# A two-layer Mamba and attention kernel: the state scan's B factor through PSUM, half of its C product on GpSimd

## The chip, the cores and the metric

One core of one Trainium2 chip runs the whole program. The metric is the device time of one execution in microseconds (us), the median of the runs shown.

## The reference, cut to what matters

The input x has shape (2, 2048, 256). It passes two layers, each `x = x + s * g`. In the first layer s is a Mamba block with a GELU feed-forward behind it, and g is the SiLU of a SwiGLU block with blockwise FP4 rounding. In the second, s is an attention over a length of 2 with 16 heads, and g is the SiLU of a chain of three blocks of linear layers with low-rank parts. The change concerns the Mamba scan, with 512 inner channels and 16 states:

```
def step(h, inp):
    dt_t, B_t, C_t, x_t = inp
    dA = jnp.exp(dt_t[..., None] * A)
    h = dA * h + dt_t[..., None] * B_t[:, None, :] * x_t[..., None]
    y = jnp.sum(h * C_t[:, None, :], axis=-1)
    return (h, y)
...
y = ys.transpose(1, 0, 2) + D * xc
y = y * _silu(z)
return y @ out_proj_w
```

B_t and C_t have 16 values for each time step, the same for all channels; they come out of a projection of xc (`x_proj_w`).

## The kernel before

The sequence is cut into 16 chunks (u = 0 to 15) of 128 time steps for both batch rows, so a chunk has T = 256 columns. Channels lie on the partitions, 512 of them as four groups m of 128. For a chunk, `head` does the layer norm, the input projection, the convolution (as matmuls with diagonal matrices, `cdiag`), the projection to dt, B and C, and the product `ux` = dt * xc. `scan` follows; `fp4_half` and `tail` do the FP4 block and the feed-forward; `second` is the whole second layer of the chunk.

`scan` goes through the 16 states in pairs: 8 steps a chunk, 128 in all. B and C were written to a small tensor in device memory (`bc`), and each step loads both, broadcast to all partitions, in one transfer (`bcs`, 128 x 1024 values). ScalarE makes `decay` = exp(dt * A) in 8 instructions. VectorE does three long instructions on 2048 columns: `hh` = ux * B, then `tensor_tensor_scan` over decay and hh, then `hh` = hh * C. TensorE sums over the states: 16 transposes of hh against the identity for each step accumulate in the two PSUM banks `y`. When all steps are done, y is multiplied with silu(z), transposed back and projected (`sz`, `y2`, `po`). `hh` and `bcs` have two buffers each.

None of this is issued where it is written. `Recorder` records every operation with its engine; a planner inside the kernel then gives each a cost and a start time, goes forward and backward through all of them in several passes with keys from two lists (`adjust`, `passes`), takes the buffers of each tag in turn, and `issue` emits the result as one fixed order for each engine. So all instructions of the kernel carry one line of the profile (L579 before; the same statement is L605 in the changed file), and they are told apart by tile names. Each engine works through its own list in order; an instruction that waits holds all that stand behind it. Loads and stores stand in the list of SyncE (SP). GpSimd (POOL) does almost nothing: `ident`, some memsets, and the inverse roots of the layer norms, `tensor_tensor` with `pow` on 2 or 4 columns (`ln_sq`, `ln_y`).

The eight PSUM banks are dealt out by `BANKS` and `USES`: two for y, two for `m` (head and the end of scan), two for `f` (FP4 and feed-forward), one for `s` and one for `h` (second layer).

Of the kernel before, what the change touches and what calls it, by code (L numbers as in the profile page):

```python
# [29 lines left out]
BANKS = {"y": 2, "m": 2, "f": 2, "s": 1, "h": 1}  # L30
USES = {
    "q": "f", "s0": "s", "s1": "s", "h0": "h", "h1": "h",
    "e0": "m", "e1": "y", "g0": "h", "g1": "f",
# [8 lines left out]
class Recorder:  # L42
# [69 lines left out]
    def cost(self, engine, method, args, kwargs):  # L112
# [6 lines left out]
        if engine == "gpsimd":  # L119
            if method == "memset":  # L120
                return 0.04
            return 0.69 if method == "tensor_tensor" else 0.19
# [88 lines left out]
    def prepare(self):  # L211
# [12 lines left out]
        for i, (engine, method, args, kwargs, stage) in enumerate(ops):  # L224
# [14 lines left out]
            if engine == "gpsimd":  # L239
                self.table[i] = int(method != "memset")  # L240
            if engine == "sync":
                self.size[i] = 2 if args[0].dtype == BF16 else 4
                for d in args[0].shape:
                    self.size[i] *= d
            if engine == "scalar" and method == "activation":
                func = str(args[2]).rsplit(".", 1)[-1]
                self.table[i] = self.TABLES.get(func, 0)
# [41 lines left out]
    def backward(self, unit, bonus, ahead):  # L289
# [7 lines left out]
        def transfer(i):  # L297
            return size[i] / self.RATE if engine[i] == "sync" else 0.0
# [68 lines left out]
    def forward(self, key, bonus, ahead):  # L367
# [10 lines left out]
        warm, upto, moved, kind = False, 0, 0.0, 0  # L378
        tags, lines, turn, opened_of = {}, {}, {}, {}
# [53 lines left out]
        while done < n:  # L433
            best_e, best_t = None, 1e18
            for e, c in cand.items():
                if c:
                    f = free[e]
                    m = min(ready[i] for i in c)
                    t = f if f > m else m
                    if t < best_t:  # L440
                        best_e, best_t = e, t
# [5 lines left out]
            for i in c:  # L447
                if ready[i] <= limit:
                    k = key[i]
                    if ready[i] > best_t:  # L450
                        k -= (ready[i] - best_t) * 0.3
# [6 lines left out]
            t = max(free[best_e], ready[i])  # L458
# [4 lines left out]
            if best_e == "gpsimd" and table[i]:  # L463

                t = max(t, free["vector"])
# [22 lines left out]
            if best_e == "sync":  # L488

                moved = max(moved, t + cost) + self.size[i] / self.RATE  # L490
                stop = moved + tails["sync"]
# [91 lines left out]
def tile_two_layers(ctx: ExitStack, tc: tile.TileContext, a: dict):  # L583
# [53 lines left out]
    def load_x(u):  # L637
        t = io.tile([P, B, D], F32, tag="xt", name=f"xt_{u}")
# [12 lines left out]
    w_xp = const.tile([P, 4, 2, 2, R], F32, tag="w_xp", name="w_xp")  # L651
    xpw = a["x_proj_w"].rearrange("(c p) (s f) -> p c s f", p=P, s=3)
    for q in range(2):
        rec.sync.dma_start(w_xp[:, :, q, 0, :], xpw[:, :, 0, :])
        rec.sync.dma_start(w_xp[:, :, q, 1, :], xpw[:, :, 1 + q, :])
# [57 lines left out]
    ddiag = const.tile([P, 4, P], F32, name="ddiag")  # L713
    for m in range(4):
        rec.vector.tensor_scalar(ddiag[:, m, :], ident, dvec[:, m : m + 1], None, ALU.mult)
    state = const.tile([P, NS, 4, B], F32, name="state")

# [123 lines left out]
    def load_second():  # L841
        wt["qkv"] = load("w_qkv", [P, 2, 3 * D], a["qkv_w"].rearrange("(c p) f -> p c f", p=P))

        rec.vector.tensor_scalar(
            wt["qkv"][:, :, 2 * D :], wt["qkv"][:, :, 2 * D :], 0.5, None, ALU.mult
        )
# [14 lines left out]
    def make_qlora_weights():  # L861

        scl = load("q_scl", [P, 6, 2, D // BLK], a["scales"].rearrange("i (c p) n -> p i c n", p=P))
        wl = const.tile([P, 6, 2, D], F32, tag="w_l", name="w_l")
        for i in range(6):
            qi = tmp.tile([P, 2, D], I32, tag="t2k_s0", name=f"qi_{i}", bufs=depth["s0"])
            rec.sync.dma_start(qi, a["qweights"][i].rearrange("(c p) d -> p c d", p=P))
            lab = t2k("s0", f"lab_{i}")
# [5 lines left out]
            for c in range(2):  # L874
                wv = w[:, c, :].rearrange("p (n k) -> p n k", k=BLK)
                rec.vector.tensor_tensor(
                    wv, wv, scl[:, i, c, :].unsqueeze(2).to_broadcast([P, D // BLK, BLK]), ALU.mult
# [23 lines left out]
    def head(u, xt):  # L901
# [51 lines left out]
        for m in range(4):  # L953
            rec.tensor.matmul(
                pd[: 4 * R, :T], lhsT=w_xp[:, m].rearrange("p a b r -> p (a b r)"), rhs=xc[:, m, :],
                start=(m == 0), stop=(m == 3),
            )
        xdbl = mam.tile([4 * R, T], F32, tag="xdbl", name=f"xdbl_{nm}", bufs=1)
        rec.scalar.copy(xdbl, pd[: 4 * R, :T])
        bc = dram.tile([2 * NS, T], F32, tag="bc", name=f"bc_{nm}")  # L960
        for q in range(2):
            rec.sync.dma_start(bc[q * NS : (q + 1) * NS, :], xdbl[(2 * q + 1) * R : (2 * q + 2) * R, :])
# [17 lines left out]
        return dict(xt=xt, xn=xn, lnt=lnt, xc=xc, dt=dt, ux=ux, bc=bc)  # L980

    def scan(u, h):
# [3 lines left out]
        y = [bank("y", f"y_{nm}_{g}") for g in range(TG)]  # L986
        for g in range(TG):
            for m in range(4):
                rec.tensor.matmul(
                    y[g][:, m * P : (m + 1) * P], lhsT=h["xc"][:, m, g * P : (g + 1) * P],  # L990
                    rhs=ddiag[:, m, :], start=(m == 0), stop=False, skip_group_check=True,
                )
        bcv = h["bc"].rearrange("(s n) t -> s n t", s=2)
        for n in range(0, NS, 2):

            bcs = scn.tile([P, 2, 2, T], F32, tag="bcs", name=f"bcs_{nm}_{n}", bufs=2)
            rec.sync.dma_start(bcs, bcv[:, n : n + 2, :].partition_broadcast(P))
# [9 lines left out]
            bn = bcs[:, 0].unsqueeze(2).to_broadcast([P, 2, 4, T])  # L1007
            cn = bcs[:, 1].unsqueeze(2).to_broadcast([P, 2, 4, T])
# [18 lines left out]
            rec.vector.tensor_tensor(hv[:, :, :P], hv[:, :, 1:], cn, ALU.mult)  # L1027
            for k in range(2):
                for g in range(TG):
                    for m in range(4):  # L1030
                        rec.tensor.matmul(
                            y[g][:, m * P : (m + 1) * P],
                            lhsT=hh[:, k, m, g, :P],
                            rhs=ident, is_transpose=True, start=False, stop=(n + k == NS - 1),
                            skip_group_check=True,
                        )

        y2 = [None] * TG
        for g in range(TG):
            pz = bank("m", f"pz_{nm}_{g}")  # L1040
            for c in range(2):
                rec.tensor.matmul(
                    pz, lhsT=h["lnt"][:, c, g * P : (g + 1) * P], rhs=w_in[:, c, DI : 2 * DI],
                    start=(c == 0), stop=(c == 1),
                )
            sz = scn.tile([P, DI], F32, tag="sz", name=f"sz_{nm}_{g}", bufs=1)
            rec.scalar.activation(sz, pz, AF.Silu)
            rec.vector.tensor_tensor(sz, y[g], sz, ALU.mult)
            pt = bank("m", f"py_{nm}_{g}").rearrange("p (m t) -> p m t", m=4)
            for m in range(4):  # L1050
                rec.tensor.transpose(pt[:, m, :], sz[:, m * P : (m + 1) * P], ident)
            y2[g] = t2k("m", f"y2_{nm}_{g}").rearrange("p (m t) -> p m t", m=4)
            rec.scalar.copy(y2[g], pt)
        po = bank("m", f"po_{nm}").rearrange("p (g d) -> p g d", g=TG)
        for g in range(TG):
            for m in range(4):
                rec.tensor.matmul(
                    po[:, g, :], lhsT=y2[g][:, m, :],
# [49 lines left out]
    def tail(u, h, x2, sgs, x1):  # L1108
# [37 lines left out]
        for g in range(TG):  # L1146
            sg = sgs[g]
            rec.vector.tensor_tensor(sg, sg, s[:, g, :], ALU.mult)
            rec.vector.tensor_tensor(x1[:, g, :], sg, h["xt"][:, g, :], ALU.add)


    def second(u, xv):
# [44 lines left out]
        rec.scalar.copy(dkv, pdkv)  # L1197
# [5 lines left out]
        bias_row(vm, 32, 2 * D, D)  # L1203
        for c in range(2):
            for bb in range(B):
                rec.tensor.matmul(
                    vm, lhsT=ht[:, c, bb * P : (bb + 1) * P], rhs=wt["qkv"][:, c, 2 * D :],
                    start=False, stop=(c == 1 and bb == B - 1),
                )
# [7 lines left out]
        rec.scalar.activation(e, e, AF.Tanh, scale=0.5 * float(BLK) ** -0.5)  # L1217
        for s in range(2):
            cs = ct[:, s * D : (s + 1) * D]
            rec.vector.tensor_tensor(  # L1220
                cs.rearrange("p (h d) -> p h d", d=BLK),
                dkv[:, D : 2 * D].rearrange("p (h d) -> p h d", d=BLK),
                e[:, s * NS : (s + 1) * NS].unsqueeze(2).to_broadcast([P, NS, BLK]), ALU.mult,
# [90 lines left out]
    for u in range(NU):  # L1314
# [9 lines left out]
        x1 = mam.tile([P, B, D], F32, tag="x1", name=f"x1_{u}")  # L1324
        tail(u, h, x2, sgs, x1)
        rec.stage = (u, SECOND)
        if u == 0:
# [6 lines left out]
        (3, 1, 2.23), (9, 3, -0.03), (15, 4, 1.53), (5, 1, -1.64), (13, 0, 0.68), (14, 4, -2.53),  # L1334
        (3, 3, -0.31), (14, 1, 0.96), (6, 2, -0.01), (11, 4, 1.22), (14, 2, 1), (11, 1, 0.05),
        (8, 0, 0.01), (2, 1, -2.41), (13, 1, 2.14), (3, 2, 0.51), (6, 3, 1.05), (0, 1, 1.16),
        (11, 0, -0.47), (5, 3, -1.29), (14, 0, 0.2), (13, 4, -0.85), (7, 2, 0.99), (12, 1, 0.89),
        (13, 3, -0.99), (1, 2, 0.28), (15, 1, 2.77), (14, 3, -1.39), (8, 1, 0.09), (7, 3, -0.25),
        (15, 3, 1.61), (6, 1, 0.87),
    ]  # L1340
    passes = [
        (20.0, 0.3, 0.0, 1.02, 0.1, [
            (9, 4, -0.033), (9, 1, 0.008), (4, 2, "gpsimd", -0.309), (1, 3, "tensor", 0.016),
            (2, 1, "gpsimd", 0.015), (1, 4, "vector", -0.12), (7, 3, "scalar", -0.018),
            (7, 3, "vector", 0.085), (1, 2, "gpsimd", 0.027), (1, 1, "gpsimd", -0.003),
            (9, 4, "gpsimd", 0.128), (11, 1, "vector", -0.088), (3, 4, "gpsimd", -0.076),
            (15, 4, "vector", 0.027), (1, 2, "scalar", -0.075), (8, 0, "vector", 0.016),
            (15, 3, "scalar", -0.469), (7, 3, -0.043), (13, 0, "vector", -0.017),
            (4, 3, "gpsimd", -0.036), (6, 4, 0.029), (8, 2, "vector", 0.849),
            (7, 0, "vector", -0.277), (9, 1, "vector", 0.009), (8, 2, "gpsimd", -0.192),  # L1350
            (1, 3, "gpsimd", -0.014), (0, 0, -0.03), (1, 1, "scalar", -0.005), (15, 2, 0.008),
            (3, 2, "scalar", 0.081), (7, 4, 0.045), (8, 3, 0.119), (2, 0, "tensor", -0.001),
# [184 lines left out]
```

## Time and profile before

| what | value |
|---|---|
| median of 3 runs | 1725.03 us (1724.42, 1725.03, 1729.31) |
| the profiled execution, its own time | 1715.39 us |
| its span, first to last instruction | 1713.5 us |
| mean granted TensorE clock | 0.963 |
| busy: VectorE, TensorE, ScalarE, GpSimd | 1614.3, 1552.3, 1419.4, 183.5 us |
| moved by DMA | 87.75 MB, 51 GB/s over the span |

The profile names the engines PE (TensorE; PEld is its weight load), DVE (VectorE), ACT (ScalarE), POOL (GpSimd) and SP (SyncE). A group is written engine, operation, out<-in, shapes and count; after the bar its busy time and the mean of one instruction in ns, and after the next bar how long the engine was idle just before these instructions and what ended that. Rows of a timeline begin with the start and the duration in us; where a row stands for x2, the duration is that of both.

### The profile page before, as it was taken

What the parts mean: (1) busy time and instruction counts of PE and PEld (TensorE: products, weight loads), DVE (VectorE), ACT (ScalarE), POOL (GpSimd) and SP (SyncE); (2) the same over time, 40 slices, a digit from 0 to 9 for tenths busy, and PEclk for the clock granted to TensorE, in tenths of its full rate; (3) what the DMA queues carried; (4) which work ended last, traced back from release to release, by engine and by line L of the source; (5) the groups of instructions that cost most, each with busy time, mean ns of one, the idle gap of its engine ahead of it and who ended that gap; (6) DMA issues with size and microseconds to landing.
All of it is one profiled execution on the core that took longest, in us unless ns stands there. A gap on an engine that the chain in (4) does not pass through costs nothing.

```text
span 1713.5 us, 21982 instructions
## 1 busy us (share of the span) xinstructions
PE 1552.3 (91%) x7948; PEld 1224.1 (71%) x7948; DVE 1614.3 (94%) x1638; ACT 1419.4 (83%) x2885; POOL 183.5 (11%) x114
## 2 busy tenths in 40 slices
PE   7736989999899999989999998999989899998997
PEld 5535758678687867768687876878677686867775
DVE  8999999999999999999999999999998999999932
ACT  5636877989899899899989898999978898897734
POOL 0000002001011201020102011001130101100100
PEclk9858989999999999999999999999999999999999
DMA  7322222313222232222222331222222132211000
GB/s 188 92 46 51 50 46 46 61 32 57 57 46 47 47 63 38 44 58 50 53 47 47 57 58 32 51 64 38 57 44 46 44 51 51 51 44 50 25 7 13
DMA packets 310666, 87.75 MB, mean 51 GB/s; under 512 B 262775, under 2 KB 276765, under 8 KB 310558
## 3 DMA queue, kind: packets, MB, share of 16 engines
q1 hardware_dynamic: 310558, 86.36, 25.5%
q8 instruction: 62, 1.02, 0.2%
q14 instruction: 46, 0.38, 0.1%
HBM read 80.62 MB, written 4.72 MB: 50 GB/s over the span
## 4 chain that ended last, share of the span: by engine, by line
PE 41%; ACT 20%; DVE 9%; issue 3%; POOL 1%; DMA 0%; POOLq 0%; ACTq 0%; SPq 0%; DVEq 0%
PE bank_f L579 16%; PE bank_m L579 8%; PE bank_s L579 7%; ACT decay L579 7%; PE bank_y L579 6%; ACT L579 6%; DVE hh L579 4%; ACT t2k_s L579 3%; PE bank_h L579 2%; DVE fp_l L579 2%; ACT t2k_f L579 1%; DVE t2k_s L579 1%; ACT dt L579 1%; POOL ln_sq_s L579 1%; ACT fp_h L579 0%
## 5 line engine op out<-in xcount | busy, mean ns | idle before, releaser
L579 DVE TENSOR_TENSOR_SCAN hh<-decay,hh 128x2064 f32<-128x2064 f32 x128 | 569.7, 4451 | 1.4 <-DVE ln_m_m L579 0.4
L579 ACT ACTIVATE decay<-dt,amat 128x256 f32<-128x256 f32 x1024 | 437.5, 500 | 34.3 <-DVE hh L579 33.0
L579 ACT ACT_TABLE_LOAD x313 | 401.6, 1283 | 16.5 <-DVE hh L579 3.9
L579 PE MATMUL bank_y<-ident,hh 128*128 128x128 f32 x2048 | 279.8, 283 | 36.1 <-DVE hh L579 36.1
L579 PEld LDWEIGHTS bank_y<-ident,hh 128*128 128x128 f32 x2048 | 246.6, 147 | 72.1 <-issue 47.1
L579 DVE TENSOR_TENSOR hh<-ux,bcs 128x2048 f32<-128x2048 f32 x128 | 291.8, 2279 | 6.7 <-PE bank_y L579 6.5
L579 DVE TENSOR_TENSOR hh<-hh,bcs 128x2048 f32<-128x2048 f32 x128 | 291.9, 2281 | 0.1
L579 POOL TENSOR_TENSOR ln_sq_s<-ln_sq_s,power 128x2 f32<-128x2 f32 x45 | 86.9, 1932 | 755.2 <-ACT ln_sq_s L579 755.2
L579 PE MATMUL bank_f<-w_f,t2k_f 128*128 128x256 f32 x512 | 133.6, 388 | 11.4 <-ACT t2k_f L579 11.3
L579 PE MATMUL bank_f<-t2k_f,w_f 128*128 128x256 f32 x512 | 127.6, 389 | 4.0 <-ACT t2k_f L579 3.3
L579 PE MATMUL bank_m<-xi,cdiag 128*128 128x256 f32 x512 | 124.8, 378 | 0.0
L579 PEld LDWEIGHTS bank_f<-w_f,t2k_f 128*128 128x128 f32 x512 | 94.3, 193 | 30.7 <-ACT t2k_f L579 17.6
L579 PEld LDWEIGHTS bank_f<-t2k_f,w_f 128*128 128x128 f32 x512 | 97.8, 194 | 21.7 <-ACT t2k_f L579 6.2
L579 PEld LDWEIGHTS bank_m<-xi,cdiag 128*128 128x128 f32 x512 | 93.6, 189 | 14.2 <-issue 0.5
L579 PE MATMUL bank_h<-t2k_s,w_l 128*128 128x256 f32 x360 | 92.0, 390 | 8.6 <-ACT t2k_s L579 8.6
L579 PE MATMUL bank_f<-w_down,hq 128*128 128x256 f32 x384 | 93.1, 386 | 6.7 <-ACT hq L579 6.5
L579 DVE SCALAR_TENSOR_TENSOR fp_l<-fp_h,fp_l 128x704 f32<-128x704 f32 (+2 forms) x124 | 91.8, 740 | 6.8 <-ACT fp_h L579 6.4
L579 PE MATMUL bank_f<-w_up,t2k_f 128*128 128x352 f32 x256 | 91.4, 475 | 6.0 <-ACT sg L579 2.9
L579 PE MATMUL bank_s<-w_qkv,t2k_s 128*128 128x256 f32 (+1 forms) x300 | 90.8, 430 | 4.1 <-DVE t2k_s L579 4.1
L579 PE MATMUL bank_f<-w_gate,t2k_f 128*128 128x352 f32 x256 | 90.0, 471 | 2.0 <-ACT h L579 2.0
L579 PE MATMUL bank_s<-w_l,t2k_s 128*128 128x256 f32 x360 | 89.3, 381 | 0.6 <-ACT t2k_s L579 0.6
L579 PEld LDWEIGHTS bank_f<-w_down,hq 128*128 128x128 f32 x384 | 71.6, 192 | 22.3 <-ACT hq L579 11.5
(172 smaller groups left out, 2434.2 us busy)
## 6 DMA issues: line engine op xcount, KB each, us to landing
bcs<-bc SPq DMA_DIRECT2D x128, 512.0 KB, 4.9
xt<-in_x_dram SPq DMA_DIRECT2D x16, 256.0 KB, 3.8
out_dram<-t2k_s SPq DMA_DIRECT2D x15, 256.0 KB, 2.2
w_f<-in_ffn_w_dram SPq DMA_DIRECT2D x2, 1024.0 KB
state<-hh SPq DMA_DIRECT2D x120, 8.0 KB, 2.9
t2k_s<-in_qweights_dram SPq DMA_DIRECT2D x6, 256.0 KB, 3.1
w_in<-in_in_proj_w_dram SPq DMA_DIRECT2D x1, 1024.0 KB, 5.1
h<-in_w_gate_dram SPq DMA_DIRECT2D x6, 128.0 KB
```

The source lines that it names most:

```text
L579: getattr(getattr(self.nc, engine), method)(*args, **kwargs)
```

## The change

- B no longer goes through device memory. The projection gives B three times (`w_xp` gets a third block), ScalarE and VectorE split the value into three bf16 parts (`three`), and in each step two bf16 matmuls with a one-hot column (`pick`) put B, broadcast over the partitions, into a PSUM bank of its own, `b`. VectorE's first product reads it there.
- The load of a step brings C alone (`cs`, half the bytes).
- The product with C is split by channels. Groups 0 and 1 stay on VectorE (1024 columns), and are transposed and summed in PSUM as before, with half of the transposes and one `y` bank. Groups 2 and 3 go to GpSimd (`prod`, one buffer), which then issues a DMA that adds prod to an accumulator in SBUF, `yc`. The first product of a chunk is written to yc directly; xc * D is added by another such DMA, and at the end a last one adds the two state halves. silu(z) for these channels is computed in their own layout (`pzc`, `szc`).
- `m` and `f` and the fifth bank share one pool `w` of four banks.
- x is loaded again for the end of layer one instead of being kept; the scales of the weights are loaded in six pieces; v uses one projection of row 0 in place of the sum of both.
- The planner knows the new costs, and lets a long GpSimd product and VectorE instructions with two SBUF inputs exclude each other. All its keys and passes are new, so the order on every engine is new.

```diff
-BANKS = {"y": 2, "m": 2, "f": 2, "s": 1, "h": 1}
+BANKS = {"y": 1, "w": 4, "s": 1, "h": 1, "b": 1}
...
             if best_e == "gpsimd" and table[i]:
-                t = max(t, free["vector"])
+                if locked:
+                    t = max(t, free["vector"])
+                if table[i] == 2:
+                    held = t + cost
+            if best_e == "vector":
+                locked = bool(table[i])
...
-    w_xp = const.tile([P, 4, 2, 2, R], F32, tag="w_xp", name="w_xp")
+    w_xp = const.tile([P, 4, 3, 2, R], F32, tag="w_xp", name="w_xp")
...
-        for q in range(2):
-            rec.sync.dma_start(bc[q * NS : (q + 1) * NS, :], xdbl[(2 * q + 1) * R : (2 * q + 2) * R, :])
+        rec.sync.dma_start(bc, xdbl[4 * R : 5 * R, :])
+        three = parts[u % 2]
+        rest = t2k("m", f"rest_{nm}")[: 6 * R, :T]
+        rec.scalar.copy(three[: 6 * R, :], pd[: 6 * R, :T])
+        rec.vector.tensor_tensor(rest, xdbl, three[: 6 * R, :], ALU.subtract)
+        rec.scalar.copy(three[2 * R : 4 * R, :], rest[2 * R : 4 * R, :])
+        rec.scalar.copy(three[4 * R : 6 * R, :], rest[4 * R :, :])
+        rec.vector.tensor_tensor(
+            three[4 * R : 6 * R, :], rest[4 * R :, :], three[4 * R : 6 * R, :], ALU.subtract
+        )
...
+        for m in range(2, 4):
+            rec.scalar.activation(xc[:, m, :], xc[:, m, :], AF.Copy, scale=dvec[:, m : m + 1])
...
-            bcs = scn.tile([P, 2, 2, T], F32, tag="bcs", name=f"bcs_{nm}_{n}", bufs=2)
-            rec.sync.dma_start(bcs, bcv[:, n : n + 2, :].partition_broadcast(P))
+            cs = scn.tile([P, 2, T], F32, tag="bcs", name=f"bcs_{nm}_{n}", bufs=2)
+            rec.sync.dma_start(cs, h["bc"][n : n + 2, :].partition_broadcast(P))
+            pb = bank("bb", f"pb_{nm}_{n}").rearrange("p (k t) -> p k t", k=2)
+            for k in range(2):
+                rec.tensor.matmul(
+                    pb[:, k, :], lhsT=pick[:, n + k : n + k + 1].to_broadcast([P, P]), rhs=three,
+                    start=True, stop=True,
+                )
...
-            bn = bcs[:, 0].unsqueeze(2).to_broadcast([P, 2, 4, T])
-            cn = bcs[:, 1].unsqueeze(2).to_broadcast([P, 2, 4, T])
+            bn = pb.unsqueeze(2).to_broadcast([P, 2, 4, T])
+            cn = cs.unsqueeze(2).to_broadcast([P, 2, 2, T])
...
-            rec.vector.tensor_tensor(hv[:, :, :P], hv[:, :, 1:], cn, ALU.mult)
+            hk = hh.rearrange("p k m b t -> p k (m b) t")
+            rec.vector.tensor_tensor(hk[:, :, :4, :P], hk[:, :, :4, 1:], cn, ALU.mult)
+            if n == 0:
+                rec.gpsimd.tensor_tensor(yk, hk[:, :, 4:, 1:], cn, ALU.mult)
+                rec.gpsimd.dma_start(yc[:, 0], xc[:, 2:], accum_op=ALU.add)
+            else:
+                prod = scn.tile([P, 2, 2, T], F32, tag="prod", name=f"prod_{nm}_{n}", bufs=1)
+                pk = prod.rearrange("p k m (b t) -> p k (m b) t", b=B)
+                rec.gpsimd.tensor_tensor(pk, hk[:, :, 4:, 1:], cn, ALU.mult)
+                rec.gpsimd.dma_start(yc, prod, accum_op=ALU.add)
             for k in range(2):
                 for g in range(TG):
-                    for m in range(4):
+                    for m in range(2):
...
+        rec.gpsimd.dma_start(yc[:, 0], yc[:, 1], accum_op=ALU.add)
...
+        sz = scn.tile([P, 2, T], F32, tag="sz", name=f"szc_{nm}", bufs=1)
+        rec.scalar.activation(sz, pz, AF.Silu)
+        y3 = yc[:, 0]
+        rec.vector.tensor_tensor(y3, y3, sz, ALU.mult)
```

## The prediction

> **What bounds the kernel now.** I read the page's busy line first, then a table of stretches, then the chain, then the groups of VectorE, and last the timeline around GpSimd's few instructions.
>
> ```profile
> PE 1552.3 (91%) x7948; PEld 1224.1 (71%) x7948; DVE 1614.3 (94%) x1638; ACT 1419.4 (83%) x2885; POOL 183.5 (11%) x114
> ...
> PE 41%; ACT 20%; DVE 9%; issue 3%; POOL 1%; DMA 0%; POOLq 0%; ACTq 0%; SPq 0%; DVEq 0%
> ```
>
> ```profile
> core 0: us, PE busy (x) PEld busy (x) DVE busy (x) ACT busy (x) POOL busy (x), PEclk, DMA share, GB/s
> ...
> 58.00:1616.00 1558.00, 1421.69 (x7347) 1126.31 (x7346) 1531.85 (x1386) 1337.85 (x2712) 172.07 (x89) 0.96 0.26 49
> 1616.00:1714.00 98.00, 83.16 (x397) 63.53 (x395) 36.11 (x89) 42.70 (x97) 7.15 (x10) 0.98 0.03 9
> ```
>
> The stretch from 58 to 1616 us holds all scan steps. VectorE is busy there for 1531.85 of 1558 us; only 26 us are idle. The chain names TensorE most (41%), but TensorE has 136 us to spare there and ScalarE 220. So VectorE sets the length of this stretch. The last 98 us are the end of the last chunk, where everything waits in turn.
>
> VectorE's three long groups, 128 of each:
>
> ```profile
> L579 DVE TENSOR_TENSOR_SCAN hh<-decay,hh 128x2064 f32<-128x2064 f32 x128 | 569.7, 4451 | 1.4 <-DVE ln_m_m L579 0.4
> L579 DVE TENSOR_TENSOR hh<-hh,bcs 128x2048 f32<-128x2048 f32 x128 | 291.9, 2281 | 0.1
> L579 DVE TENSOR_TENSOR hh<-ux,bcs 128x2048 f32<-128x2048 f32 x128 | 291.8, 2279 | 6.7 <-PE bank_y L579 6.5
> L579 DVE TENSOR_TENSOR h<-h,bank_f 128x352 f32<-128x352 f32 x64 | 32.3, 509 | 9.6 <-PE bank_f L579 9.2
> ...
> L579 DVE TENSOR_TENSOR ux<-dt,xc 128x1024 f32<-128x1024 f32 x16 | 19.3, 1208 | 3.1 <-ACT dt L579 3.1
> ```
>
> Now what GpSimd does beside VectorE. A `pow` on two columns takes 0.69 to 0.70 us in the quiet end of the run, but its mean over 45 is 1.93. The timeline shows why:
>
> ```profile
> 1274.02 2.29 DVE L579 TENSOR_TENSOR hh<-hh,bcs 128x2048 f32<-128x2048 f32 x1
> 1274.39 9.58 POOL L579 TENSOR_TENSOR ln_sq_s<-ln_sq_s,power 128x2 f32<-128x2 f32 x1 [9.20 <-ACT ln_sq_s L579]
> 1276.22 2.29 DVE L579 TENSOR_TENSOR hh<-ux,bcs 128x2048 f32<-128x2048 f32 x1
> 1278.42 0.69 DVE L579 SCALAR_TENSOR_TENSOR fp_l<-fp_h,fp_l 128x512 f32<-128x512 f32 x1
> 1279.03 4.46 DVE L579 TENSOR_TENSOR_SCAN hh<-decay,hh 128x2064 f32<-128x2064 f32 x1
> 1283.39 0.67 DVE L579 SCALAR_TENSOR_TENSOR fp_l<-fp_h,fp_l 128x512 f32<-128x512 f32 x1
> ```
>
> Five VectorE instructions with two inputs in SBUF stand in a row, and the small pow ends only at 1283.97, behind four of them. GpSimd with SBUF operands waits while VectorE reads two SBUF operands, and here it does not get in between two of these.
>
> **The change, part by part.** The counts are those of the two built orders.
>
> VectorE. The C product shrinks from 128 x 2.281 = 291.9 us to 128 x 1.208 (the 1024-column row `ux`) = 154.6: minus 137.3. The B product keeps its columns but reads B in PSUM; a product with a PSUM input costs what one from SBUF does (509 ns for 352 columns, 1208 for 1024: a slope of 1.04 ns each), so it stays at 2.28. Added are 16 + 16 small subtractions for the split (about 0.41 each, as rows of 256 columns): plus 13. The other exchanges cancel. Net **-124 us**, all of it on the engine that sets the stretch.
>
> TensorE. 1152 transposes fewer; the 2048 into y took 279.8 us, 0.137 each: -157. 256 bf16 matmuls of 256 columns are new; rows of that shape took 282 ns alone, and the pipelined floor by the transposes' row would be 0.14: +36 to +72. The v projection saves 32, about -8. Net -95 to -130. Since TensorE does not set the stretch, I count this as nothing. If VectorE stopped being the bound, TensorE's 1422 minus about 110 would still be the lower of the two.
>
> ScalarE. 13 table loads fewer (313 to 300 in the built order, 1283 ns each: -17), 32 copies of 512 columns fewer (-19), 80 small ones more (0.37 to 0.5 each: +34). About zero, and hidden.
>
> GpSimd's product. No row shows a long one. Its small rows give a slope: a memset of 128 columns took 204 ns and one of a single column 100 (0.8 ns a column, no input); the affine select of 128 columns took 292 (1.5 ns, one input). One more input by the same step makes 2.2 ns, so 1024 columns cost about **2.35 us**; the bounds are 1.6 (as if one input) and 3.2 (twice that). The page "GPSIMD Engine Reference" (section 3.1) has 4497 ns for 2048 columns of a two-input add, so half of it, 2.25, would be an estimate by that page; it warns that elementwise work there is about twice as slow as on VectorE.
>
> Where does it run? After each scan I took the built VectorE order and looked for the first run of instructions that don't read two SBUF operands, priced by the rows above. In 78 of 128 cases this run lasts 2.0 us or more, mostly because it is the next B product, which now has one SBUF input: 2.20 us from start to start. In 50 cases it is short, 0.84 us on average (a reduce, a statistics row, a feed-forward product). If GpSimd holds VectorE's next two-input instruction until it is done, 0.1 us of start included, the 50 short ones cost 1.6 us each and the long ones little more than 0.1: 90 us in all. At 3.2 us the same count gives 168 to 180; at 1.6 it gives 43.
>
> The trace shows only one direction, GpSimd waiting for VectorE: after the pow that ends near 835.5 us the scan that had started at 835.26 is no longer than others, 4.44. So the hold costs between 0 and 180; I take the middle count, 90, minus 20 that fall into the 26 us in which VectorE is idle anyway: **+70**. The page "SBUF — State Buffer" (Who interferes with whom) says that whoever comes first has the shared port pair for the whole instruction and the other fully blocks; it speaks against this change, and by it the full count of holds stands, and without it the sum would fall by 70.
>
> The accumulating DMA. 128 products each need one on POOL's queue (112 of 512 KB, 16 of xc), plus 16 of 256 KB at the chunk ends. `prod` has one buffer, so product n+1 waits until DMA n has landed; behind it on POOL wait the pows, and hh's next B product on VectorE waits for product n-2. No row shows an accumulate; the nearest are these (KB, us from issue to landing):
>
> ```profile
> bcs<-bc SPq DMA_DIRECT2D x128, 512.0 KB, 4.9
> ...
> state<-hh SPq DMA_DIRECT2D x120, 8.0 KB, 2.9
> ...
> w_in<-in_in_proj_w_dram SPq DMA_DIRECT2D x1, 1024.0 KB, 5.1
> ```
>
> It reads 1 MB (prod and yc) and writes half; I take 5.5, with 4.5 (the shortest bcs) and 9.8 (twice its median) as bounds. With 2.35 for the product, about 1 for the issue on POOL (SP's take 0.36 to 0.61) and 0.4 for two signals, one round is 9.2 us. Scans stand 11.1 us of VectorE work apart on average in the built order, but 42 of 127 gaps are under 9, and one step of buffering covers them. So 0; it decides from a round of about 12 us on, that is a landing over 8.2.
>
> B through PSUM. The new wait: bank `b` is single, so the two matmuls of the next step stand behind the B product of this one and before the next. A scan of 4.4 us lies between mostly, TensorE needs 0.3 to 0.6 and what is queued ahead of it: **+10**, bounds 0 and 50 (0.4 a step). C's smaller load and SP's equal list (391 and 398 instructions) count nothing. One y bank and a common pool: a chunk's first y matmul now waits for the last `sz`; the transposes can run a step late, zero, bounds -10 and +20.
>
> The end. Behind the last scan come product, accumulate, the last 256 KB accumulate and the y3 product, about 2.4 + 1 + 5.5 + 1 + 4 + 1 = 15 us; before, x2 came 24 us after the last scan. Mostly covered: **+5**, bounds 0 and 16.
>
> **Sum.** 1713.5 - 124 + 70 + 10 + 5 = 1674.5 span; 1.9 lie around it: 1676.4. The median of the runs is 9.6 above the profiled execution (1725.03 against 1715.39): **1686 us**. The measurement tells about 0.3%, 5 us, from no change.
>
> **Rivals.** (a) The accumulates become the loop: POOL's round of product, issue, landing decides as soon as it exceeds about 12 us. At a landing of 9.8 it is 13.6; 127 x 13.6 = 1727, plus 58 ahead and 100 behind, plus 11.5: about 1896, and at 8.5 some 1725. For it: one buffer, twice the reads, the other transfers on the same engines. Against: DMA is at 26% in the stretch, and 1 MB landed in 5.1. (b) The hold costs more than it saves: at 3.2 us and all gaps short by the count, 168 in place of 70 and 30 for B: 1804. For it: the 9.58 us row, and by the same pricing, two-input instructions are still 990 of the 1481 us of VectorE's work in the built order. (c) VectorE is not held at all, and the 70 vanish: 1616. For it: the scan of 4.44. (d) The gap between cost and saving just closes: no change.
>
> **How the numbers follow.** My case 0.48 (own range 1650 to 1718), (c) 0.10, (a) 0.16, (b) 0.20, (d) 0.06. Faster is the first two, 0.58; same 0.06; slower 0.36. For 8 in 10 I leave out the lower half of (c) and the upper parts of (a) and (b), which reach from 1725 up: 1620 to 1800.
>
> **What would show it.** Right: VectorE's busy near 1490 plus rows lengthened by holds; the C group at 128 x 1.2 us; POOL's product near 2.35 where it starts with a B product. Wrong: POOL waiting on the accumulate in most steps with landings over 8 us and VectorE idle "until POOL" (a); scan rows with a mean well over 5 us (b); scan rows still at 4.45 everywhere (c); VectorE idle for bank b by more than 50 us (the +10).

## The result, and the profile after

The changed kernel takes 1731.2 us (median of 20 runs, 1727.81 to 1735.92), the kernel before 1724.72 in the 20 runs beside it: a ratio of 1.0040, 95% interval 1.0021 to 1.0058. It is slower by 0.4%. I had forecast 1686, a gain of 2.3%.

The profiled execution has a span of 1732.3 us against 1713.5, and a mean granted clock of 0.943 against 0.963. These are the busy line and the chain of the changed kernel:

```profile
PE 1462.8 (84%) x7052; PEld 1140.0 (66%) x7052; DVE 1615.5 (93%) x1673; ACT 1418.6 (82%) x2936; POOL 580.7 (34%) x386
...
DVE 31%; PE 15%; issue 11%; ACT 8%; POOL 3%; DMA 1%; DVEq 0%; ACTq 0%; POOLq 0%; SPq 0%
```

TensorE lost 90 us. VectorE, which was to lose 124, is as busy as before: 1615.5 against 1614.3. The table of stretches, cut 3 us ahead of the first scan and 3 us behind the last as for the kernel before, says the same:

```profile
48.00:1635.00 1587.00, 1353.72 (x6570) 1058.68 (x6568) 1543.59 (x1464) 1350.94 (x2795) 568.39 (x360) 0.94 0.40 72
1635.00:1733.00 98.00, 76.64 (x353) 58.87 (x353) 33.94 (x82) 45.20 (x96) 9.27 (x13) 0.93 0.08 19
```

The stretch with all scan steps is 29 us longer than before. VectorE is idle for 43 us of it, not 26, and busy for 12 more; the stretch begins 10 us earlier, which is why the span grew by 19 only. The end takes 98 us, as before. Where the 124 us went is in VectorE's groups:

```profile
L605 DVE TENSOR_TENSOR_SCAN hh<-decay,hh 128x2064 f32<-128x2064 f32 x128 | 573.7, 4482 | 3.6 <-ACT decay L605 0.9 <-ACT hh L605 0.3
L605 DVE TENSOR_TENSOR hh<-ux,bank_b 128x2048 f32<-128x2048 f32 x128 | 291.0, 2273 | 11.0 <-PE bank_y L605 5.5 <-PE bank_b L605 3.5 <-issue 1.4
L605 DVE TENSOR_TENSOR hh<-hh,bcs 128x1024 f32<-128x1024 f32 x128 | 178.7, 1401 | 0.2
L605 DVE SCALAR_TENSOR_TENSOR fp_l<-fp_h,fp_l 128x704 f32<-128x704 f32 x68 | 70.8, 1040 | 5.8 <-ACT fp_h L605 5.0
...
L605 DVE TENSOR_SCALAR fp_sc<-fp_sc 128x44 f32<-128x44 f32 x34 | 18.1, 533 | 0.7
...
L605 DVE SCALAR_TENSOR_TENSOR ln_m_m<-ln_mv_m,ln_y_m 128x2 f32<-128x2 f32 x32 | 13.3, 433 | 1.1 <-POOL ln_y_m L605 1.1
...
L605 DVE BATCH_NORM_STATS2 ln_st_f<-x 128x6 f32<-128x256 f32 x32 | 12.1, 408 | 0.1
```

The product with an input in the PSUM bank and the statistics row take what they took. The half C product has a mean of 1401 ns where 1024 columns cost 1208, the 704-column fp_l row 1040 (882 before), a tensor_scalar of 44 columns 533 (177) and a row of two columns 433 (149). The last two do next to no work. Their rows in the kernel before were:

```profile
L579 DVE SCALAR_TENSOR_TENSOR fp_l<-fp_h,fp_l 128x704 f32<-128x704 f32 x68 | 60.0, 882 | 4.7 <-ACT fp_h L579 4.6
...
L579 DVE TENSOR_SCALAR fp_sc<-fp_sc 128x44 f32<-128x44 f32 x34 | 6.0, 177 | 0.0
...
L579 DVE SCALAR_TENSOR_TENSOR ln_m_m<-ln_mv_m,ln_y_m 128x2 f32<-128x2 f32 x32 | 4.7, 149 | 0.9 <-POOL ln_y_m L579 0.9
```

The timeline of both engines in the changed kernel shows what lengthens them:

```profile
1094.42 0.68 DVE L605 TENSOR_TENSOR fp_l<-fp_l,fp_sc 128x512 f32<-128x512 f32 x1
1095.03 0.15 DVE L605 SCALAR_TENSOR_TENSOR ln_m_s<-ln_mv_s,ln_y_s 128x2 f32<-128x2 f32 x1
1095.06 2.17 POOL L605 TENSOR_TENSOR prod<-hh,bcs 128x1024 f32<-128x1024 f32 x1
1095.10 3.22 DVE L605 TENSOR_TENSOR hh<-hh,bcs 128x1024 f32<-128x1024 f32 x1
...
1097.53 0.90 POOL L605 DMA_DIRECT2D yc<-prod  x1 [0.30 <-POOL prod L605]
1098.24 2.27 DVE L605 TENSOR_TENSOR hh<-ux,bank_b 128x2048 f32<-128x2048 f32 x1
```

GpSimd's product starts at 1095.06; VectorE's C product, which starts 0.04 us later, takes 3.22 us: 2.13 of waiting until GpSimd's product has ended, then 1.09, close to its own 1.2.

To count this I took, from the trace, each VectorE row beside a GpSimd product and subtracted the median of the rows of its form that stand beside none. The sum is **113 us**, and 72 of the 128 products have over 0.3 us of it beside them. I call the sum the held time below. The product itself and its DMA came out much as priced. From GpSimd's groups:

```profile
L605 POOL TENSOR_TENSOR prod<-hh,bcs 128x1024 f32<-128x1024 f32 x112 | 270.1, 2412 | 595.8 <-DVE hh L605 506.0 <-DVE fp_sc L605 17.7 <-DVE h L605 11.2
L605 POOL DMA_DIRECT2D yc<-prod x112 | 99.1, 885 | 34.6 <-POOL prod L605 28.4 <-DVE fp_l L605 3.2 <-DMA bcs<-bc 2.3
```

and from the DMA issues, with KB each and the median from issue to landing:

```profile
yc<-prod POOLq DMA_DIRECT2D x112, 512.0 KB, 5.0
```

That is 2.41 us a product and 5.0 us from issue to landing. The idle time ahead of the products ends with VectorE's `hh` (506 of 596 us), that is, with the scan; a DMA is not among its three named releasers.

### The profile page after: what moved, and what is told of

It reads as the page before. It is cut to its first block, busy times and chain, and to the rows that moved or that the text cites. A ratio compares the mean times of both kernels' runs of the same rounds, so it can differ in the third digit from the quotient of the medians.

```text
span 1732.3 us, 20920 instructions
## 1 busy us (share of the span) xinstructions
PE 1462.8 (84%) x7052; PEld 1140.0 (66%) x7052; DVE 1615.5 (93%) x1673; ACT 1418.6 (82%) x2936; POOL 580.7 (34%) x386
## 4 chain that ended last, share of the span: by engine, by line
DVE 31%; PE 15%; issue 11%; ACT 8%; POOL 3%; DMA 1%; DVEq 0%; ACTq 0%; POOLq 0%; SPq 0%
DVE hh L605 18%; PE bank_w L605 9%; DVE fp_l L605 4%; PE bank_s L605 3%; ACT L605 3%; DVE t2k_s L605 2%; ACT decay L605 2%; DVE fp_sc L605 2%; PE bank_y L605 1%; PE bank_h L605 1%; POOL ln_sq_s L605 1%; ACT t2k_s L605 1%; DVE h L605 1%; ACT t2k_f L605 1%; POOL yc L605 1%
## 5 line engine op out<-in xcount | busy, mean ns | idle before, releaser
L605 DVE TENSOR_TENSOR_SCAN hh<-decay,hh 128x2064 f32<-128x2064 f32 x128 | 573.7, 4482 | 3.6 <-ACT decay L605 0.9
L605 POOL TENSOR_TENSOR prod<-hh,bcs 128x1024 f32<-128x1024 f32 x112 | 270.1, 2412 | 595.8 <-DVE hh L605 506.0
L605 DVE TENSOR_TENSOR hh<-ux,bank_b 128x2048 f32<-128x2048 f32 x128 | 291.0, 2273 | 11.0 <-PE bank_y L605 5.5
L605 PE MATMUL bank_y<-ident,hh 128*128 128x128 f32 x1024 | 151.6, 289 | 48.6 <-DVE hh L605 48.4
L605 DVE TENSOR_TENSOR hh<-hh,bcs 128x1024 f32<-128x1024 f32 x128 | 178.7, 1401 | 0.2
L605 PEld LDWEIGHTS bank_y<-ident,hh 128*128 128x128 f32 x1024 | 126.8, 149 | 73.5 <-DVE hh L605 40.5
L605 PE MATMUL bank_w<-w_f,t2k_f 128*128 128x256 f32 x512 | 133.1, 390 | 7.1 <-ACT t2k_f L605 7.0
L605 PE MATMUL bank_w<-t2k_f,w_f 128*128 128x256 f32 x512 | 128.7, 392 | 5.0 <-ACT dt L605 1.6
L605 PE MATMUL bank_w<-xi,cdiag 128*128 128x256 f32 x512 | 122.3, 385 | 1.1 <-ACT xi L605 1.0
L605 POOL DMA_DIRECT2D yc<-prod x112 | 99.1, 885 | 34.6 <-POOL prod L605 28.4
L605 PE MATMUL bank_w<-w_down,hq 128*128 128x256 f32 x384 | 99.6, 389 | 7.9 <-ACT hq L605 7.8
```

The costliest lines, as they stand in the source:

```text
L605: getattr(getattr(self.nc, engine), method)(*args, **kwargs)
```

## Experiments

Three theories stood at first. **H**: the saving is real and the held time pays it back. **A**: the accumulating DMAs and the single prod buffer set the pace. **O**: the new order is slower by itself, and the held time falls into slack. Each ratio is against runs of the kernel before on the same chip.

**Short products (e1_short).** The planned order stays; at issue the product is cut.

```diff
+ args = [args[0][:, :1, :1], args[1][:, :1, :1], args[2][:, :1, :1, :P], *args[3:]]
```

> The planned order of the changed kernel is kept instruction for instruction; each of the 128 GpSimd products of h and C covers 128 of its 1024 columns (prod and yc are cleared once, so the other columns hold zeros or old sums: the output is wrong by that). The accumulating DMAs keep their size. Theory H (the port hold pays the saving back): in the changed kernel's trace 72 of the 128 products have a lengthened VectorE instruction beside them, 113 us in all. With a product of some 0.5 us the holds nearly go: VectorE busy 1500 to 1520 instead of 1615.5, the scan stage shorter by 80 to 115, median 1615 to 1655. Theory A (the accumulating DMAs, their landing and the single prod buffer set the pace): the round of GpSimd is 1.9 shorter but its DMA is unchanged; under 20 us gained. Theory O (the planned order itself, with its new matmuls and one bank fewer for each stream, is slower by what it is, and the holds fall into slack): VectorE busy falls by 100 and its idle time rises by as much; median 1715 to 1735.

Measured: 1637.4 us, ratio 0.950 (0.945 to 0.955). The busy line, and from VectorE's groups the C product and the 44-column row:

```profile
PE 1431.4 (88%) x7041; PEld 1124.7 (69%) x7052; DVE 1511.5 (92%) x1673; ACT 1413.7 (86%) x2936; POOL 363.2 (22%) x389
```

```profile
L613 DVE TENSOR_TENSOR hh<-hh,bcs 128x1024 f32<-128x1024 f32 x128 | 156.6, 1228 | 0.2
...
L613 DVE TENSOR_SCALAR fp_sc<-fp_sc 128x44 f32<-128x44 f32 x34 | 6.1, 181 | 0.7
```

VectorE is 104 us less busy and the kernel 94 us faster; the C product is back at 1228 ns and the 44-column row at 181. The idle time did not take up what the holds gave back. H holds; A and O are off by over 70 us.

**No accumulating DMA (e2_noacc).**

```diff
- rec.gpsimd.dma_start(yc, prod, accum_op=ALU.add)
```

> The same order with the 112 accumulating DMAs of yc<-prod left out (the sums of the GpSimd channels over the states are then missing; the products run in full, and the two small accumulates of each unit stay). Theory H: the products still hold the port, VectorE busy stays within 20 us of 1615 and the median within 1715 to 1735; a product may start a little earlier where it waited for the buffer. Theory A: without the DMAs the loop is free of the landing of 5.0 us, median 1620 to 1680. Theory O: no change.

Measured: 1732.0 us, ratio 1.0055 (1.0026 to 1.0083), VectorE busy 1617.0, held time 114 us. Without 112 DMAs of 512 KB nothing moves: A is out.

**The product on VectorE (e3_vector).**

```diff
- rec.gpsimd.tensor_tensor(pk, hk[:, :, 4:, 1:], cn, ALU.mult)
+ rec.vector.tensor_tensor(pk, hk[:, :, 4:, 1:], cn, ALU.mult)
```

> The same order, but the 1024-column product of the GpSimd channels is issued on VectorE at the same place of the order, into the same prod buffer, and the accumulating DMAs follow it as before; nothing is left out. This undoes the one part that holds the port, and keeps B in PSUM, the DMAs and the fewer transposes. Theory H: VectorE takes 128 x 1.21 = 155 us more and loses the 113 us of holds, so it is about 40 busier and the median is 1745 to 1785: the split is worth 40, not 155. If the holds cost nothing (theory O) the whole 155 shows, 1850 to 1890. Theory A gives the same 1850 or more, as the accumulating DMAs are still there.

Measured: 1745.2 us, ratio 1.0122 (1.0071 to 1.0172). The busy line, and the product in its new place among VectorE's groups:

```profile
PE 1470.0 (84%) x7041; PEld 1145.1 (66%) x7052; DVE 1642.0 (94%) x1801; ACT 1420.2 (81%) x2936; POOL 279.7 (16%) x258
```

```profile
L607 DVE TENSOR_TENSOR prod<-hh,bcs 128x1024 f32<-128x1024 f32 x112 | 136.1, 1215 | 2.9 <-DMA yc<-prod 2.8
```

The products cost VectorE 128 x 1.215 = 156 us, yet it is only 26 busier, since the 113 us of holds are gone and rows overlap by 125 us in place of 108. Moving half of the C product to GpSimd was worth 14 us as this kernel is ordered, and 108 in e1_short, where GpSimd's products are an eighth as wide and 6 us are still held (1745.2 to 1637.4).

So the hold is the cause. But the planner knows of it: it marks the VectorE instructions that a product would shut out, by their inputs in SBUF, as needing the port, and keeps them out of a product's time. The others it takes as port-free. Why does it fail? The first suspicion was its view of the DMA. In the planner's own start times, pairing each product with its own scan, 65 of 128 begin more than 1.2 us after the end of the scan, most of them because `prod` is not yet free; in the trace 17 do (the expectation below has 59 and 16). Port-free work then stands where no product runs.

**The DMA's cost in the plan (e4_plan).** The two constants are set by the profile, and the list of passes is searched anew.

```diff
-                return 1.1
+                return 0.9
-                    self.size[i] *= 1.3
+                    self.size[i] *= 0.75
```

> Nothing of the computation is changed; only the order is planned anew. The changed kernel's planner takes an accumulating DMA for an issue of 1.1 us and a transfer 1.3 times its bytes; the profile shows an issue of 0.885 us and a landing of 5.0 us, so the two constants become 0.9 and 0.75, and the list of passes is searched anew for this cost. Theory P (the holds come from a planned order that expects a product to start late, when the prod buffer comes free, and puts the port-free instructions there, while on the chip it starts 92 ns after its scan): in the planner's own start times 59 of 128 products of the changed kernel begin over 1.2 us after the end of the scan before them, in the trace 16. With the products expected where they fall, the lengthened rows come down from 113 us to 20 to 50 and the median to 1650 to 1690, under both kernels. Rival (the hold is in the mix of VectorE's work, most of which needs the port, and no order has enough port-free work beside 128 products): 90 to 120 us of lengthened rows again, median 1715 to 1740.

Measured: 1717.6 us, ratio 1.0002 (0.9990 to 1.0014), VectorE busy 1589.5, held time 82 us. It lies between the two expectations in held time, and in the rival's range by its median. The holds are fewer, but the 14 us of time are less than another list of passes can make (e8_second below), so how much of them is the DMA's cost is not shown.

**A later landing (e5_late).** The chip is moved towards the plan instead of the plan towards the chip.

```diff
+ rec.gpsimd.dma_start(spill, prod)
  rec.gpsimd.dma_start(yc, prod, accum_op=ALU.add)
```

> The order of the changed kernel, with one more DMA on GpSimd's queue ahead of each of the 112 accumulating ones: the same 512 KB of prod are copied to device memory and not used. It makes the accumulate land some 2 to 4 us later and costs GpSimd another issue of 0.885 us, so more products wait for the prod buffer, as the plan expected. Theory P: the products move towards the places that the plan has for them, the lengthened rows fall from 113 to 60 to 95 us, and the kernel gets no slower for its slower DMA: median 1700 to 1735. Theory A (accumulates as the loop): later landings delay the next product and with it hh and the scan: 1760 to 1950.

Measured: 1732.4 us, ratio 1.0079 (1.0049 to 1.0109). The accumulate lands after 6.2 us, 66 products start over 0.3 us behind their scan where 44 did, and the held time is 105 us. A slower DMA cost nothing that is clear of the noise, against A once more; but the holds hardly fell, so a product that is late is not thereby where the plan wants it. P's figure for it missed.

What is in the held rows of e4_plan? fp_l<-fp_h,fp_l has 21.1 us, the C product 17.4, sg<-sg,t2k_f 11.4, fp_sc 7.9. In three of these four, all but the C product, one input is the very view that is written. The line that marks an instruction as needing the port leaves out such an input:

**The marks (e6_marks).** As e4_plan, and the marks count inputs that are also the output; the passes are searched anew.

```diff
-                    v for v in (*args[1:], *kwargs.values())
-                    if hasattr(v, "tensor") and v is not out and self.space(v.tensor) != PSUM
+                    v for v in (*args[1:], *(v for k, v in kwargs.items() if k not in ("out", "accum_out")))
+                    if hasattr(v, "tensor") and self.space(v.tensor) != PSUM
```

> Nothing of the computation is changed; the order is planned anew with the costs of the run before and one line more. The planner marks a VectorE instruction as needing the port by its inputs in SBUF, and leaves out an input that is the same view as the output, so 400 instructions that work in place (the scan, fp_l<-fp_h,fp_l, sg<-sg,t2k_f, t2k_s<-t2k_s,t2k_s, fp_sc<-fp_sc) pass as port-free: 575 are marked, 975 would be. Of the 82 us of lengthened rows in the run before, the five groups just named hold 47 (21.1, 11.4, 7.9, 3.8 and the scan's 2.5); of the changed kernel's 113 us they hold 45. Theory M (the holds are those of a plan that does not see them): with all 975 marked the lengthened rows come to 15 to 45 us and the median to 1655 to 1695, under the kernel before. Rival (VectorE has too little port-free work beside its products, so that a better plan only turns holds into idle time): VectorE's busy time falls but its idle time rises by as much, median 1705 to 1730.

Measured: **1653.9 us, ratio 0.9631 (0.9608 to 0.9655)**, held time 32 us, the median just under M's range. Busy line, chain, the scan stretch and the C group:

```profile
PE 1448.2 (88%) x7052; PEld 1142.8 (69%) x7052; DVE 1533.2 (93%) x1673; ACT 1469.0 (89%) x2978; POOL 578.4 (35%) x386
...
PE 44%; ACT 24%; DVE 23%; issue 7%; POOL 1%; DMA 1%; DVEq 0%; SPq 0%; ACTq 0%; POOLq 0%
```

```profile
38.00:1551.00 1513.00, 1342.32 (x6577) 1061.96 (x6578) 1462.74 (x1466) 1400.25 (x2835) 566.24 (x360) 0.94 0.42 76
```

```profile
L605 DVE TENSOR_TENSOR hh<-hh,bcs 128x1024 f32<-128x1024 f32 x128 | 160.5, 1255 | 1.5 <-DMA bcs<-bc 1.1
```

The same instructions, with the same 128 products of 2.38 us, in another order: VectorE is 82 us less busy than in the changed kernel. In 87 cases the product now runs beside a B product, where 52 did. The stretch with the scan steps is 74 us shorter, with VectorE idle for 50 us of it. This version beats both kernels, and its chain is no longer led by VectorE.

**Controls.** The marks alone, with the old DMA cost (e7_marks_only):

> Only the marks are mended (975 port instructions instead of 575); the accumulating DMA keeps the changed kernel's cost (issue 1.1, 1.3 times its bytes), and the list of passes is searched anew. Theory M (marks alone do it): lengthened rows 20 to 50 us, median 1650 to 1690. Theory M+P (both are needed: with the DMA costed too long the plan still expects many products late, and its port-free stretches stand where no product runs): lengthened rows 60 to 100, median 1690 to 1725.

Measured: 1701.8 us, ratio 0.988 (0.984 to 0.992), held time 56 us. The median lies in the range of M+P, the held time between the two ranges. By this run the marks alone do not bring all of the gain; that is one list only.

Both mends with another list of passes (e8_second):

> Both mends as in e6_marks, with another list of passes from the same search begun at another seed. It tells how much of the 1654 is the luck of one list: if the mends are what counts, the lengthened rows come to 20 to 50 us and the median to 1650 to 1690; if it was the list, the median is anywhere from 1660 to 1740.

Measured: 1675.9 us, ratio 0.973 (0.969 to 0.977), held time 48 us. The held time is within the range of the mends, near its end; the median lies in both ranges, so it does not decide. Some 22 us are the luck of a list. That bears on e7_marks_only too: it is 26 us slower than this run with 8 us more held, and 20 us of that is VectorE idle for longer (140 us against 120). Whether the DMA's cost is needed beside the marks is therefore open. That the marks count is not: all three lists made with them (1654, 1676, 1702) are faster than both made without (1718, 1731), and have less held (32 to 56 us against 82 and 113).

The short products again, in the order of e6_marks (e9_short6):

> The order of e6_marks, with the GpSimd products cut to 128 of 1024 columns as in e1_short (the output is wrong by that). In e6_marks 32 us of rows are still lengthened beside the products. If they lie on the path, the median falls by 20 to 32 to 1622 to 1634; if VectorE's work beside them has slack by now, by less than 10. In the changed kernel's order the same cut was worth 94.

Measured: 1639.9 us, ratio 0.952 (0.947 to 0.956), VectorE busy 1502.8. The cut is worth 14 us here and 94 in the changed kernel's order; of the 32 us still held, about half lies on the path, between the two cases that I had named.

The kernel before with passes searched anew (e10_before), as a guard against crediting the search:

```diff
- passes = [... the old list ...]
+ passes = [... a list searched in the same way ...]
```

> The kernel before, with nothing changed but its list of passes, which is searched anew from nothing in the same way and for the same time as those of the four re-planned kernels. Rival (the new search is simply better than the old lists, whatever the marks): the median falls here too, to 1660 to 1700. Theory M (the gain is the change's own, once the plan sees the port): no gain, 1710 to 1740.

Measured: 1724.5 us, ratio 1.0056 (1.0039 to 1.0073) to the 1716.8 of the kernel before on that chip. This search, one list of it, gains the kernel before nothing, and e4_plan was searched in the same way with the old marks. So what e6_marks gains is not the search's.

| order planned with | old DMA cost | DMA cost by the profile |
|---|---|---|
| the old marks (575) | 113 us held, 1731.2 | 82 us held, 1717.6 |
| all marks (975) | 56 us held, 1701.8 | 32 us held, 1653.9 (48 and 1675.9 with another list) |

## Why the prediction was wrong

The sum was 1713.5 - 124 + 70 + 10 + 5 = 1674.5 for the span, and 1732.3 came. By its terms:

- **VectorE's instructions, -124: right.** The counts before and after, each at the mean of its undisturbed rows, differ by -124.4 us. B from PSUM costs 2273 ns a product (2.28 predicted), the C half without holds 1.22.
- **GpSimd's product, 2.35: right** (2.41, and 2.16 where nothing is in its way); the bounds of 1.6 and 3.2 were wide of it on both sides. The step behind it was a little high: e1_short's products of 128 columns took 0.44 us at the least, which with 2.16 makes 1.92 ns a column, as an estimate, where 2.2 was taken.
- **The hold, +70: the step that failed.** It was 113 us. The mechanism and its price were right (113 us over 72 is 1.57 each; 1.6 predicted); the count had two faults. It let every product start with the end of its scan. 84 of 128 did, within 0.3 us, with 61 us of held time beside them, in line with the count's rate of 90 for 128 (59 for 84). The other 44 start later, and beside 32 of these a row is held as well, for 54 us (a few rows stand beside two products and count for both). And it took off 20 us as falling into idle time. Little or nothing did: VectorE's idle time grew, and in e1_short 104 us less of busy time made 94 us less of time.
- **B through PSUM, +10, and the end, +5: right in sum by luck, not in place.** The span outside VectorE's busy time went from 99.2 to 116.8 us, +17.6. All of it lies in the stretch with the scans; the end takes 98 us as before, so its +5 was nothing. Bank b ended only 3.5 us of idle ahead of the B products, where 10 were taken; bank y ended 5.5, no more than before (6.5). What grew in that stretch besides are gaps under 0.15 us, from 2.7 to 8.6 us in all, and waits for ScalarE, for `h` above all (6 us).
- **Not in the sum: 11 us of overlap.** A VectorE row mostly starts some 85 ns before the row ahead of it ends; the rows of before overlap by 119.7 us in all, those of the changed kernel by 108.5. The loss is in chains like reduce, fp_sc, reciprocal, fp_l, which the new order puts back to back: such a row starts some 35 ns after the end of the one it reads from.

43 more for the hold, 11 for the overlap and 3 for idle time make 57 of the 57.8 us between forecast and span; the rest is rounding.

The page "SBUF — State Buffer" (Who interferes with whom) spoke against the change with its rule that the first to come has the port pair for the whole instruction. By it I had said that the full count stands. Row 1095.10 agrees, with 2.13 of its 3.22 us spent waiting, and the full 90 without the 20 taken off would have been nearer, though still short of 113. The page "GPSIMD Engine Reference" (section 3.1) gave an estimate of 2.25 us for 1024 columns; the trace's mean is 2.41, with waits.

Of the rivals, (a) is refuted by e2_noacc and e5_late. (c) is refuted as well, and what it would have given (1616) is 21 us under what e1_short measured with the holds nearly gone (1637). (b) put the price too high: the scans' mean is 4482 ns. (d), cost and saving just closing, is nearest to what came; I had given it 0.06, and my own chance of slower rested on (a) and (b), which are not how it came.

The prediction also took the order as given. What the runs showed beyond it is that the order was the fault that could be mended: 400 VectorE instructions that work in place passed in it as port-free, and the forms of them that came behind the start of a product were held (fp_l and the scan by up to 1.98 us).

## What to carry to other kernels

Work moved to GpSimd is paid for by the VectorE instructions that stand beside it, not by its own length: list what will be beside each piece, from when it can really start, and count every instruction that is shut out, the two-column ones and those that work in place among them. Where a planner or a hand-written order keeps such work apart, compare its marks and its start times with the trace before judging the idea: here the same instructions took 1731 us in one order and 1654 in another. And do not let a stall on the busiest engine fall into its idle time unless you can say which wait it replaces.

## What the runs showed of the hardware

- A GpSimd product of 1024 fp32 columns with both inputs in SBUF takes 2.16 us where nothing is in its way (2.41 in the mean, up to 3.41). Meanwhile a VectorE instruction with two inputs in SBUF that starts behind it waits, however short: a two-column row took 2.13 us. Where VectorE's row starts first, GpSimd's product is the longer one: 3.21 us behind a C product of 1.23 us that had begun 0.06 us ahead of it.
- A tensor_scalar from SBUF to SBUF waits too, with one tensor input: 533 ns in the mean of all 34 rows of 44 columns, 13 of which stand beside a product, and 181 in e1_short. Not lengthened beside products were the product with an input in PSUM (2273 ns), the reduce over 704 columns (879), the statistics (408 to 412) and the reciprocal (421).
- GpSimd does get in between two VectorE instructions that both need the port, as at 1095.06 behind the row ln_m_s. The row of 9.58 us in the kernel before, where it stood behind several, is not how it always goes; what decides was not tried.
- An accumulating DMA of 512 KB from SBUF to SBUF landed 5.0 us after its issue, which took GpSimd 0.885 us; behind a copy of the same size on its queue 6.2 us.
